# The beginning of an attention stage: order of norm, sigma and key preparation, and how far ahead they run

## The chip, the cores and the metric

The kernel runs on one core of a Trainium2 chip. A core has five engines that run their own instruction streams: TensorE (PE, matmuls; PEld is its weight load), VectorE (DVE), ScalarE (ACT), GpSimd (POOL) and SyncE (SP, which here only issues DMAs). ScalarE issues DMAs too. The metric is the device time of one execution in microseconds; the figure for a kernel is the median of its runs. One execution was recorded by the hardware profiler.

## The reference

A block of four residual stages on x of shape (2, 2048, 256) in float32: causal attention with 16 heads of 16, a mixture-of-experts feed-forward, a small gated stage, and the feed-forward once more, each on a layer norm of x. The change lies in the first stage only:

```python
def sn_dense(x, W, u, sigma_param):
    v = W @ u
    v = v / norm(v)
    u2 = W.T @ v
    u2 = u2 / norm(u2)
    sigma = einsum('c,cd,d->', v, W, u2)
    return x @ (sigma_param[0] / sigma * W)

h = layernorm(x)
q, k, v = split(sn_dense(h, W_qkv, u_qkv, sigma_qkv), 3)
att = einsum('bhqd,bhkd->bhqk', q, k) * hd ** -0.5
att = softmax(where(causal == 0, big_neg, att))
x = x + sn_dense(einsum('bhqk,bhkd->bhqd', att, v), W_proj, u_proj, sigma_proj)
```

sigma is a scalar per weight matrix; the kernel works out one factor sigma_param / sigma for qkv and one for proj, and applies it where results leave PSUM.

## The kernel before

x is held in eight chunks of 512 tokens (`X[0..7]`, four a batch). Attention works in **units** (batch, chunk, head group of 4 heads), 32 of them, in the list `units`. Names: `b`, `c`, `g`; `LAST` is chunk 0 of batch 1, which comes last in its batch and is prepared during the last chunk of batch 0.

For each chunk: `stat_steps` (lines 103 to 108) takes mean and variance on VectorE and 1/sqrt by a `pow` on GpSimd; `norm_steps` (L116) writes the normed tokens `xn` with four instructions, on GpSimd in attention; `flip_steps` (L126, L129) transposes them on PE into `xnT` by two PSUM banks, copied by ScalarE.

For each unit: `prepare` makes one PSUM bank of queries and keys (`psk`, L267), ScalarE writes the queries `qT` (L277, scaled by `fq`) and the keys to `sk` (L279), and SyncE copies the keys by four small DMAs into their place in a `kT` tile (L286), which GpSimd has filled with a constant row pattern the first time that it is used (L282). For group 0 of a chunk `prepare` begins with norm and transposes. `make_v` (L293, L298) makes the values of a chunk.

`Maxima` finds each query's largest score: matmuls `psm` (L333), reduced by VectorE (L342 on the diagonal, L347 elsewhere). `shift` (L351 to L358) puts the negated maximum into a row of `qT` by a transpose on VectorE and four DMAs. `softmaxes` then repeats the scores as `st` (L378), ScalarE takes exp (L382, `pt`), GpSimd clears what lies above the diagonal (L385, the mask selects), `values` multiplies with the values (`o`, L397), ScalarE copies out (L406) and GpSimd accumulates (L408). `finish` (L415 to L421) divides, `project` (L436 to L451) multiplies with W_proj and adds to x.

The main loop of attention emits all this in an order written out in the source: in each turn (`tick`) one step of the softmax of unit `na` and one step of the maxima of a later unit `nm`, with one step of the preparation of unit `nm` + 1 and of the statistics two units ahead of the chunk's need put between, and one DMA of the list `later` (loads of chunks 2 to 7, then zeros written to DRAM for a later stage). `ready` lets a softmax begin LAG turns after its maxima. `manual_schedule` makes the emitted order the order on each engine; ahead of it, a scheduler of the framework chose the order.

`spectral` works out a factor: two reductions of W times u on VectorE (L205), matmuls with one column (`psr`, L211), sums by a matmul with ones (`pss`, L224), and a chain of one-column operations on VectorE with one `pow` on GpSimd (L228 to L233). For qkv it stands behind the norm and the transposes of the first chunk and ahead of its first `psk`; for proj it is emitted at one place, at the end of the maxima of unit 1.

PSUM: four single banks (`ps_m`) serve `flip`, `psk`, `psm`, `psv`, `o` and the rest in turn, two double ones (`ps_st`) serve `st`.

The loads at the start: chunks 0 and 1 of x on SyncE's queue, W_qkv, u_qkv and sigma_qkv on ScalarE's.

Of the kernel before, what the change touches and what calls it, by code (L numbers as in the profile page):

```python
# [8 lines left out]
F32 = mybir.dt.float32  # L9
# [7 lines left out]
P = 128  # L17
D = 256
# [5 lines left out]
CH = 512  # L24
NB = CH // P
NCH = N // CH
# [15 lines left out]
WORDS = -(-EB // FW)  # L42
QTS = 6
KTS = NG * (NCH + 1)
LOW = -3e38
LAG = 3

# [2 lines left out]
def hybrid_block(  # L50
# [34 lines left out]
    def load_x(c):  # L85
        return X[c], x[c * CH:(c + 1) * CH, :].rearrange("(n p) d -> p n d", p=P)

    for c in range(2):
        nc.sync.dma_start(*load_x(c))

    ident = const.tile([P, P], F32, tag="ident", name="ident")
    make_identity(nc, ident)
# [19 lines left out]
    def norm_steps(xc, xn, nm, stats=None, eng=None):  # L112

        mv, rs = stats or (yield from stat_steps(xc, nm))
        for i in range(NB):
            (eng or nc.vector).tensor_scalar(  # L116
                xn[:, i, :], xc[:, i, :], mv[:, i, 0:1], rs[:, i:i + 1], ALU.subtract, ALU.mult
            )
        yield 1
# [16 lines left out]

    with tc.tile_pool(name="aw", bufs=1) as aw, ExitStack() as aw_ctx:

        maskq = aw.tile([P, CH], F32, tag="maskq", name="maskq")
        nc.gpsimd.memset(maskq, 0.0)  # L140
        nc.gpsimd.affine_select(
# [26 lines left out]
        KT = []  # L168
        for i in range(KTS):
            t = aw.tile([P, CH], F32, tag=f"kT{i}", name=f"kT{i}")  # L170
            KT.append(t)

        V = []
# [19 lines left out]
            return w, u, sp  # L193

        loaded = load_w(wqkv, uqkv, sqkv, 3 * D, "qkv")
        w_qkv = loaded[0]
        ones = aw.tile([P, P], F32, tag="ones", name="ones")
        nc.gpsimd.memset(ones, 1.0)

        def spectral(w, u, sp, cols, nm, bank):  # L200

            n = cols // P
            v = aw.tile([P, 2], F32, tag=f"v_{nm}", name=f"v_{nm}")
            for c in range(2):
                nc.vector.tensor_tensor_reduce(  # L205
                    wide(f"t_{nm}_{c}")[:, 0:cols], w[:, c, :], u, 1.0, 0.0, ALU.mult, ALU.add, v[:, c:c + 1]
                )
            ps = bank(f"psr_{nm}")
            for m in range(n):
                for c in range(2):  # L210
                    nc.tensor.matmul(  # L211
                        ps[:, m:m + 1], w[:, c, m * P:(m + 1) * P], v[:, c:c + 1],
                        start=c == 0, stop=c == 1,
                    )
            r = aw.tile([P, n], F32, tag=f"r_{nm}", name=f"r_{nm}")
            nc.vector.tensor_copy(r, ps[:, 0:n])

            s = aw.tile([P, 2], F32, tag=f"s_{nm}", name=f"s_{nm}")
            nc.vector.tensor_mul(v, v, v)
            nc.vector.tensor_mul(r, r, r)  # L220
            nc.vector.reduce_sum(s[:, 0:1], v, axis=AX.X)
            nc.vector.reduce_sum(s[:, 1:2], r, axis=AX.X)
            ps = bank(f"pss_{nm}")
            nc.tensor.matmul(ps[:, 0:2], ones, s, start=True, stop=True)  # L224

            f = aw.tile([P, 1], F32, tag=f"f_{nm}", name=f"f_{nm}")
            ru = aw.tile([P, 1], F32, tag=f"ru_{nm}", name=f"ru_{nm}")
            nc.vector.reciprocal(f, ps[:, 0:1])  # L228
            nc.vector.tensor_mul(f, f, ps[:, 1:2])
            nc.gpsimd.tensor_tensor(ru, f, nhalf[:, 0:1], ALU.pow)  # L230
            nc.vector.tensor_mul(f, f, ru)
            nc.vector.reciprocal(f, f)
            nc.vector.tensor_mul(f, f, sp)  # L233
            return f

        with ExitStack() as ac:
            xnp = ac.enter_context(tc.tile_pool(name="xnp", bufs=1))
# [7 lines left out]
            ps_m = ac.enter_context(tc.tile_pool(name="ps_m", bufs=4, space=PSUM))  # L245

            xnT, kT, qT, otok = {}, {}, {}, {}
            factors, nk, stats = {}, [0], {}

            order = [[0, 1, 2, 3], [1, 2, 3, 0]]  # L250
            LAST = (1, 0)
# [1 line left out]
            def bank(nm):  # L253
                return ps_m.tile([P, CH], F32, tag="mm", name=nm)

            def prepare(b, c, g):

                if g == 0:
                    xn = xnp.tile([P, NB, D], F32, tag="xn", name=f"xna_{b}_{c}")
                    yield from norm_steps(  # L260
                        X[b * NCH + c], xn, f"a{b}_{c}", stats.pop((b, c)), nc.gpsimd
                    )
                    t = xnT[b, c] = xtp.tile([P, 2, CH], F32, tag="xnT", name=f"xnTa_{b}_{c}")
                    yield from flip_steps(xn, t, bank, f"a{b}_{c}")
                ps = bank(f"psk_{b}_{g}_{c}")
                for d in range(2):
                    nc.tensor.matmul(  # L267
                        ps, w_qkv[:, d, g * P:(g + 1) * P], xnT[b, c][:, d, :],
                        start=d == 0, stop=d == 1,
                    )  # L270

                held = (b, c) == LAST
                qT[b, g, c] = qtp.tile(
                    [P, CH], F32, tag=f"qT{g}" if held else "qT", name=f"qT_{b}_{g}_{c}",
                    bufs=1 if held else QTS,
                )
                nc.scalar.activation(qT[b, g, c], ps, AF.Identity, scale=factors["q"])  # L277
                sk = skp.tile([P, CH], F32, tag="sk", name=f"sk_{b}_{g}_{c}")
                nc.scalar.activation(sk, ps, AF.Identity, scale=factors["k"])  # L279
                t = kT[b, g, c] = KT[nk[0] % KTS]  # L280
                if nk[0] < KTS:
                    nc.gpsimd.tensor_copy(t, kbias.to_broadcast([P, CH]))  # L282
                nk[0] += 1
                for j in range(4):
                    o = 32 * j + HD
                    nc.sync.dma_start(t[o - HD:o, :], sk[o:o + HD, :])  # L286
                yield
# [164 lines left out]

            units = [(b, c, g) for b in range(B) for c in order[b] for g in range(NG)]

            def preparations(n):

                todo = [units[n + 1]] if n + 1 < len(units) else []
                todo = [u for u in todo if u[:2] != LAST]
                if units[n][:2] == (0, NCH - 1):
                    todo.append((*LAST, units[n][2]))  # L460
                return (
                    (s for u in todo for s in prepare(*u)),
                    sum(4 if u[2] == 0 else 1 for u in todo),
                )


            ahead = {}
            for n in range(len(units)):
                for u in ([units[n + 1]] if n + 1 < len(units) else []) + [
                    (*LAST, units[n][2])  # L470
                ] * (units[n][:2] == (0, NCH - 1)):
                    if u[2] == 0 and (u[:2] != LAST or n < NG * NCH):
                        ahead[n - 2] = u[:2]

            def statistics(b, c):
                stats[b, c] = yield from stat_steps(X[b * NCH + c], f"a{b}_{c}", True)

            def make_vs(b, c):

# [21 lines left out]

            ready, mx, sm, behind = {}, None, None, None
            nm, na = 0, 0

            ac.enter_context(tc.manual_schedule())
            for _ in statistics(*units[0][:2]):
                pass
            first = prepare(*units[0])
            for _ in range(3):
                next(first)  # L510
            f = factors["k"] = spectral(*loaded, 3 * D, "qkv", bank)
            factors["q"] = aw.tile([P, 1], F32, tag="fq", name="fq")
            nc.vector.tensor_mul(factors["q"], f, qsel)
            for _ in first:
                pass
            for t in V:
                nc.gpsimd.memset(t, 1.0)
            loaded = load_w(wproj, uproj, sproj, D, "proj")
            w_proj = loaded[0]
            coming, steps, stat = iter(()), 0, iter(())  # L520
            while na < len(units) or due or behind:
                cols, n_m = CH, CH
                run_a = na < len(units) and ready.get(na, tick[0] + 1) <= tick[0]
                run_m = nm < len(units) and nm - na < QTS - 1
                if run_a:
                    u = units[na]
                    if sm is None:
# [39 lines left out]
                                after(5 + k, project, u[0], u[1], i, box)  # L567
                if run_m:
                    small_set = n_m <= 256 or not run_a
                    if steps and (small_set or steps == 4 or mx.left <= steps + 1):  # L570
                        next(coming, None)
                        steps -= 1
                    elif small_set:
                        next(stat, None)
                    if nm == 1 and not mx.left:
                        factors["p"] = spectral(*loaded, D, "proj", bank)
                    if later:
                        nc.sync.dma_start(*later.pop(0))
                    if not mx.left:
                        shift(*w, mx.part, nmax[nm % 2])  # L580
                        ready[nm] = tick[0] + LAG
                        mx, nm = None, nm + 1
# [702 lines left out]
```

## Time and profile before

| | |
|---|---|
| median of 3 runs | 2157.02 us (2152.82 to 2159.84) |
| profiled execution | 2150.73 us, its span 2148.8 us |
| busy: PE, weight loads | 2026.7 us (94%), 1091.1 us (51%) |
| busy: DVE, ACT, POOL | 1384.1 us (64%), 1074.9 us (50%), 872.9 us (41%) |
| chain that ended last, by engine | PE 80%, DVE 7%, POOL 4%, issue 4%, ACT 3%, DMA 1% |
| mean granted clock of TensorE | 0.979 |
| attention, its last `exp` | about 1172 us |
| first statistics, first transpose, first `psm` | 7.78, 13.45, 32.93 us |

The profile gives for each engine the time in which it was busy, in stretches that can be chosen; for groups of instructions their number, busy time and the mean of one; and for each wait what ended it ("<-"). The chain that ended last is followed back from the last instruction to what released it, step by step. The granted clock is the share of its full rate that PE was given. A busy PE isn't PE at its peak, since matmuls are pipelined.

### The profile page before, as it was taken

The page shows a single profiled execution, that of the slowest core. Times are in us where ns is not written, and L with a number is a line of the kernel's source. Part 1 is how long each engine was busy: PE and PEld are TensorE (multiplying, and loading weights), DVE is VectorE, ACT ScalarE, POOL GpSimd, SP SyncE. Part 2 cuts the span into 40 slices and gives each one's busy share as a digit, 9 for nine tenths or more (in the row PEclk, how much of TensorE's full clock was granted, in tenths as well). Part 3 has the DMA queues.
Part 4 walks back from the last instruction along what each step waited for, and adds up shares of the span by engine and source line. Part 5 has one row for each costly group of instructions (what it writes and reads, how often), then busy time and mean ns, then how long its engine had stood idle before and what let it go on. Part 6 is the DMA issues. An engine that isn't in the chain of part 4 may idle for free.

```text
span 2148.8 us, 36170 instructions
## 1 busy us (share of the span) xinstructions
PE 2026.7 (94%) x11840; PEld 1091.1 (51%) x11840; DVE 1384.1 (64%) x3424; ACT 1074.9 (50%) x1566; POOL 872.9 (41%) x1157
## 2 busy tenths in 40 slices
PE   6899999999999999999999999999999999999993
PEld 3444444444444444444444566665656566655662
DVE  2567777777676777777871455545777368763643
ACT  0437577757776757767876122233353234341330
POOL 3325344524444434434445263603432753336305
PEclk9899999999999999999999999999999999999997
DMA  2111110000000000000000511323210332103524
GB/s 93 48 49 36 45 51 16 7 6 6 3 7 6 6 4 4 6 4 4 2 2 1 217 61 64 136 76 118 84 40 25 114 112 85 35 30 131 173 73 122
DMA packets 87587, 113.04 MB, mean 53 GB/s; under 512 B 16368, under 2 KB 75120, under 8 KB 87280
## 3 DMA queue, kind: packets, MB, share of 16 engines
q1 hardware_dynamic: 74000, 75.60, 11.1%
q0 software_dynamic: 12288, 33.57, 4.7%
q8 instruction: 101, 1.65, 0.3%
q10 hardware_dynamic: 1120, 1.57, 0.2%
q14 instruction: 78, 0.64, 0.1%
HBM read 54.59 MB, written 51.64 MB: 49 GB/s over the span
## 4 chain that ended last, share of the span: by engine, by line
PE 80%; DVE 7%; POOL 4%; issue 4%; ACT 3%; DMA 1%; DVEq 0%; SPq 0%; POOLq 0%; ACTq 0%
PE st L378 15%; PE o L397 13%; PE psm L333 13%; PE eu L1060 10%; PE s L986 7%; PE ed L1084 5%; PE sy L1003 4%; PE psk L267 3%; PE tr L1045 2%; PE psz L936 1%; PE psj L446 1%; POOL xs L868 1%; PE psv L293 1%; DVE junk L342 1%; PE psl L736 1%
## 5 line engine op out<-in xcount | busy, mean ns | idle before, releaser
L382 ACT ACTIVATE pt<-st 128x1024 f32<-128x1024 f32 (+3 forms) x640 | 555.8, 895 | 189.8 <-PE psm L333 129.9
L333 PE MATMUL psm<-kT,qT 32*128 32x512 f32 (+3 forms) x2560 | 627.1, 570 | 15.0 <-DMA kT<-sk 8.9
L378 PE MATMUL st<-qT,kT 32*128 32x512 f32 (+3 forms) x2560 | 610.7, 557 | 1.3 <-ACT pt L382 1.3
L347 DVE TENSOR_REDUCE part<-psm 128x1 f32<-128x512 f32 x768 | 477.4, 682 | 121.5 <-PE psm L333 117.3
L408 POOL TENSOR_TENSOR oa<-oa,op 128x512 f32<-128x512 f32 (+3 forms) x288 | 312.8, 1086 | 454.4 <-ACT op L406 454.4
L378 PEld LDWEIGHTS st<-qT,kT 32*128 32x128 f32 x2560 | 266.1, 186 | 225.9 <-ACT pt L382 137.8
L342 DVE CUSTOM_DVE_ANT_0 junk<-psm,maskq 128x384 bf16<-128x384 f32 (+3 forms) x512 | 250.8, 490 | 112.0 <-PE psm L333 47.7
L333 PEld LDWEIGHTS psm<-kT,qT 32*128 32x128 f32 x2560 | 276.1, 186 | 86.2 <-issue 27.1
L397 PE MATMUL o<-pt,v 128*32 128x512 f32 (+3 forms) x2560 | 304.2, 545 | 12.1 <-DVE part L347 5.6
L1060 PE MATMUL eu<-we,turned 128*128 x560 | 263.7, 593 | 0.0
L1067 ACT ACTIVATE es<-ea 128x256 f32<-128x256 f32 x156 | 65.0, 417 | 357.9 <-DVE ea L1065 357.8
L986 PE MATMUL s<-xT_f,ws 128*128 128x512 f32 x512 | 231.4, 595 | 0.0
L895 POOL DMA_INDIRECT yg<-ys,slot x128 | 128.1, 1001 | 234.3 <-DVE x L908 74.0
L385 POOL TENSOR_SCALAR_AFFINE_SELECT pt<-pt 128x256 f32<-128x256 f32 x256 | 102.3, 407 | 211.6 <-ACT pt L382 207.7
L406 ACT COPY op<-o 128x512 f32<-128x512 f32 (+3 forms) x288 | 148.3, 515 | 64.1 <-PE o L397 48.8
L1065 DVE TENSOR_TENSOR ea<-eu,be 128x512 f32<-128x512 f32 x156 | 107.4, 688 | 111.0 <-PE eu L1060 110.4
L1084 PE MATMUL ed<-we,turned 128*128 x624 | 162.6, 383 | 14.5 <-ACT turned L1050 14.5
L397 PEld LDWEIGHTS o<-pt,v 128*32 128x32 f32 x2560 | 52.5, 108 | 218.0 <-DVE part L347 123.4
L1084 PEld LDWEIGHTS ed<-we,turned 128*128 128x128 f32 x624 | 116.2, 190 | 87.9 <-issue 48.3
L868 POOL DMA_INDIRECT xs<-xn_f,slot x128 | 124.7, 974 | 85.1 <-DVE slot L822 57.9
L986 PEld LDWEIGHTS s<-xT_f,ws 128*128 128x128 f32 x512 | 94.8, 191 | 102.0 <-issue 95.4
L1060 PEld LDWEIGHTS eu<-we,turned 128*128 128x128 f32 x560 | 97.6, 191 | 75.0 <-issue 73.1
(266 smaller groups left out, 2111.0 us busy)
## 6 DMA issues: line engine op xcount, KB each, us to landing
xs<-xs SPq DMA_DIRECT2D x156, 128.0 KB
ys<-ey SPq DMA_DIRECT2D x156, 128.0 KB
xs<-zeros SPq DMA_DIRECT2D x78, 128.0 KB
we<-in_we_dram SPq DMA_DIRECT2D x8, 768.0 KB
x<-in_x_dram SPq DMA_DIRECT2D x8, 512.0 KB
kT<-sk SPq DMA_DIRECT2D x128, 32.0 KB
out_dram<-x SPq DMA_DIRECT2D x8, 512.0 KB
be<-in_be_dram SPq DMA_DIRECT2D x1, 3072.0 KB
```

The costliest lines, as they stand in the source:

```text
L333: nc.tensor.matmul(ps[:, :n], self.q[r, i * P:(i + 1) * P], kT[b, g, kc][r, :n], start=True, stop=True,)
L342: nc.vector.tensor_tensor_reduce(junk[:, :n], ps[:, :n], maskq[:, CH - n:], 1.0, LOW, ALU.add, ALU.max, m,)
L347: nc.vector.reduce_max(m, ps[:, :n], axis=AX.X)
L378: nc.tensor.matmul(st[:, i, off:], k[r, ks], q[r, off:], start=True, stop=True)
L382: nc.scalar.activation(pt[:, :, off:], st[:, :, off:], AF.Exp)
L397: nc.tensor.matmul(o[32 * j:32 * j + 32, off:], V[kb // NB][:, kb % NB, 4 * g + j, :], pts[j // 2][:, j % 2, off:], start=True, stop=True,)
L406: nc.scalar.copy(t[:, off:], o[:, off:])
L408: nc.gpsimd.tensor_tensor(a[:, off:], a[:, off:], t[:, off:], ALU.add)
L868: ins = nc.gpsimd.indirect_dma_start(out=XS[b], out_offset=bass.IndirectOffsetOnAxis(ap=slots[f, b][:, k, n:n + 1], axis=0), in_=xhat[f, b ...
L986: nc.tensor.matmul(ps, w[:, d, cs], xT[:, d, :], start=d == 0, stop=d == 1)
L1060: nc.tensor.matmul(ps, t[:, 1, d * P:(d + 1) * P], we_s[:, bass.ds(v + d * CH, CH)], start=d == 0, stop=d == 1,)
L1084: nc.tensor.matmul(ps[:, 0:D], t[:, 0, d * P:(d + 1) * P], we_s[:, bass.ds(v + 2 * CH + d * D, D)], start=d == 0, stop=d == 1,)
```

## The change

- x's chunk 0 is loaded in two halves of two blocks each; chunk 1 goes to ScalarE's queue, behind W_qkv, u_qkv and sigma_qkv.
- The written-out order begins at the start of attention and not ahead of the main loop.
- The first eight `kT` tiles are filled at the start.
- `spectral` becomes a generator of three steps (reductions; `psr` and sums; `pss` and the rest). For qkv the first step comes ahead of the first norm and the second ahead of the transposes; for proj one step is taken in each of three turns of unit 2.
- The norm moves from `prepare` into `statistics`, so a chunk is normed where its statistics are done; the first chunk's by VectorE, the others by GpSimd.
- While fewer than EARLY (8) units have begun, `prepare` runs for unit `nm` + 2 and not `nm` + 1 (units 0 and 1 both ahead of the loop), and maxima may be four units ahead of the softmax, not five.

```diff
+KTE = 8
+EARLY = 8
...
-    for c in range(2):
-        nc.sync.dma_start(*load_x(c))
+    for h in range(2):
+        t, src = load_x(0)
+        nc.sync.dma_start(t[:, 2 * h:2 * h + 2, :], src[:, 2 * h:2 * h + 2, :])
...
+        aw_ctx.enter_context(tc.manual_schedule())
...
             t = aw.tile([P, CH], F32, tag=f"kT{i}", name=f"kT{i}")
+            if i < KTE:
+                nc.gpsimd.tensor_copy(t, kbias.to_broadcast([P, CH]))
...
         loaded = load_w(wqkv, uqkv, sqkv, 3 * D, "qkv")
+        nc.scalar.dma_start(*load_x(1))
...
-        def spectral(w, u, sp, cols, nm, bank):
+        def spectral(w, u, sp, cols, nm, bank, got):
...
+            yield 1
             ps = bank(f"psr_{nm}")
...
             nc.vector.reduce_sum(s[:, 1:2], r, axis=AX.X)
+            yield 1
             ps = bank(f"pss_{nm}")
...
-            return f
+            got(f)
+            yield 1
...
                 if g == 0:
-                    xn = xnp.tile([P, NB, D], F32, tag="xn", name=f"xna_{b}_{c}")
-                    yield from norm_steps(
-                        X[b * NCH + c], xn, f"a{b}_{c}", stats.pop((b, c)), nc.gpsimd
-                    )
+                    xn = normed.pop((b, c))
...
-                if nk[0] < KTS:
+                if KTE <= nk[0] < KTS:
                     nc.gpsimd.tensor_copy(t, kbias.to_broadcast([P, CH]))
...
+            def coming_to(n):
+
+                if n == EARLY:
+                    return []
+                k = n + 1 + (n < EARLY)
+                return units[k:k + 1]
+
             def preparations(n):
 
-                todo = [units[n + 1]] if n + 1 < len(units) else []
-                todo = [u for u in todo if u[:2] != LAST]
+                todo = [u for u in coming_to(n) if u[:2] != LAST]
...
-                    sum(4 if u[2] == 0 else 1 for u in todo),
+                    sum(3 if u[2] == 0 else 1 for u in todo),
...
-                        ahead[n - 2] = u[:2]
+                        ahead[n - 2 + (u[:2] == LAST)] = u[:2]
 
             def statistics(b, c):
-                stats[b, c] = yield from stat_steps(X[b * NCH + c], f"a{b}_{c}", True)
+                s = yield from stat_steps(X[b * NCH + c], f"a{b}_{c}", True)
+                xn = normed[b, c] = xnp.tile([P, NB, D], F32, tag="xn", name=f"xna_{b}_{c}")
+                if not (b or c):
+
+                    next(sigma)
+                yield from norm_steps(
+                    X[b * NCH + c], xn, f"a{b}_{c}", s, nc.gpsimd if b or c else nc.vector
+                )
...
-            ac.enter_context(tc.manual_schedule())
+            def scaled(f):
+                factors["k"] = f
+                factors["q"] = aw.tile([P, 1], F32, tag="fq", name="fq")
+                nc.vector.tensor_mul(factors["q"], f, qsel)
+
+            sigma = spectral(*loaded, 3 * D, "qkv", bank, scaled)
             for _ in statistics(*units[0][:2]):
                 pass
+            next(sigma)
             first = prepare(*units[0])
-            for _ in range(3):
-                next(first)
-            f = factors["k"] = spectral(*loaded, 3 * D, "qkv", bank)
-            factors["q"] = aw.tile([P, 1], F32, tag="fq", name="fq")
-            nc.vector.tensor_mul(factors["q"], f, qsel)
+            next(first)
+            for _ in sigma:
+                pass
             for _ in first:
                 pass
+            for _ in prepare(*units[1]):
+                pass
...
+            sigma = spectral(*loaded, D, "proj", bank, lambda f: factors.update(p=f))
...
-                run_m = nm < len(units) and nm - na < QTS - 1
+                run_m = nm < len(units) and nm - na < QTS - 1 - (nm < EARLY)
...
-                    if steps and (small_set or steps == 4 or mx.left <= steps + 1):
+                    if steps and (small_set or steps == 3 or mx.left <= steps + 1):
                         next(coming, None)
                         steps -= 1
                     elif small_set:
                         next(stat, None)
-                    if nm == 1 and not mx.left:
-                        factors["p"] = spectral(*loaded, D, "proj", bank)
+                    if nm == 2:
+                        next(sigma, None)
```

In the new order PE runs `psr`, the first four transposes, `pss`, the other four, `psk` of unit 0, `psk` of unit 1, then the first `psm`.

More of the change, by code (lines that the diff above doesn't have):

```diff
@@ L247, in hybrid_block @@
             xnT, kT, qT, otok = {}, {}, {}, {}
-            factors, nk, stats = {}, [0], {}
+            factors, nk, normed = {}, [0], {}
             order = [[0, 1, 2, 3], [1, 2, 3, 0]]
@@ L468, in hybrid_block @@
             for n in range(len(units)):
-                for u in ([units[n + 1]] if n + 1 < len(units) else []) + [
-                    (*LAST, units[n][2])
-                ] * (units[n][:2] == (0, NCH - 1)):
+                for u in coming_to(n) + [(*LAST, units[n][2])] * (units[n][:2] == (0, NCH - 1)):
                     if u[2] == 0 and (u[:2] != LAST or n < NG * NCH):
-                        ahead[n - 2] = u[:2]
+                        ahead[n - 2 + (u[:2] == LAST)] = u[:2]
             def statistics(b, c):
-                stats[b, c] = yield from stat_steps(X[b * NCH + c], f"a{b}_{c}", True)
+                s = yield from stat_steps(X[b * NCH + c], f"a{b}_{c}", True)
[5 more added lines that the diff above has]
+                )
             def make_vs(b, c):
```

## The prediction

> **What bounds the kernel now.** I read the page first (TensorE, PE, is busy 94% of the span and carries 80% of the chain that ended last), then the busy time by stretches, to find where PE is not full.
>
> ```profile
> 0.00:130.00 130.00, 98.17 (x524) 50.92 (x528) 58.40 (x228) 38.59 (x63) 45.73 (x77) 0.88 0.22 70
> 130.00:870.00 740.00, 723.32 (x5428) 333.52 (x5420) 550.92 (x1330) 501.44 (x678) 306.00 (x382) 0.99 0.06 16
> ```
>
> Columns: length, busy time of PE, weight loads, VectorE, ScalarE, GpSimd, then granted clock. From 130 us on attention leaves PE idle for 16.7 us in 740; before that it is idle for 31.8 us in 130. So the change works where time is to be had, and what it saves there is kept, because all later work stands behind it on a full PE. Next the timeline and the chain of waits of that stretch:
>
> ```profile
> 12.16 4.85 POOL L116 TENSOR_SCALAR xna<-x,lnmv_a,lnrs_a 128x256 f32<-128x256 f32 x4
> 18.19 5.12 PE L211 MATMUL psr_qkv<-v_qkv,w_qkv 128*128 128x1 f32 x24
> 24.40 3.76 PE L267 MATMUL psk<-xnTa,w_qkv 128*128 128x512 f32 x4
> 32.93 2.84 PE L333 MATMUL psm<-kT,qT 32*128 32x512 f32 x8 [4.76 <-DMA kT<-sk]
> ...
> 68.01 1.81 PE psr_proj L211 x8
> ...
> 70.44 0.60 PE pss_proj L224 x2
> ...
> 92.45 0.33 PE L126 MATMUL flip_a<-ident,xna 128*128 128x128 f32 x1 [0.88 <-POOL xna L116]
> ...
> 109.28 1.62 PE L333 MATMUL psm<-kT,qT 32*128 32x256 f32 x5 [4.09 <-DMA kT<-sk]
> ```
>
> Four losses are seen: the head runs in series up to 32.93; sigma of proj holds PE between 68.0 and 70.95; the second chunk's transposes wait for GpSimd's norm, four times; the second chunk's first keys wait 4.09 us for their copy. Between them the clock drops:
>
> ```profile
> 44.00:53.50 9.50, 9.32 (x26) 6.06 (x24) 3.74 (x19) 0.00 (x0) 0.00 (x0) 0.50 0.68 227
> 64.50:74.00 9.50, 7.56 (x41) 4.44 (x44) 5.66 (x33) 2.59 (x4) 2.89 (x6) 0.50 0.32 105
> 95.00:98.00 3.00, 3.00 (x17) 1.22 (x16) 0.62 (x1) 1.18 (x2) 1.21 (x3) 0.50 0.00 0
> 109.00:115.00 6.00, 5.72 (x22) 2.79 (x23) 1.73 (x8) 1.07 (x2) 1.36 (x3) 0.50 0.10 29
> ```
>
> Before 43.7 us the record says 1.0, but four psk matmuls take 3.76 us there and 1.98 at 55.75: PE is at half rate from its start to 53.5.
>
> **The change, part by part.** Unit means one (batch, chunk, head group); the maxima of unit n are psm, its softmax st, exp and o.
>
> *x in halves, x1 to ScalarE's queue.* All statistics start at 7.78 and end with lnve at 10.2 (four blocks of 0.57 us, then 0.17). In halves, two blocks run before the second half lands. [...] I take **1.1**: lnve ends at 9.07. ScalarE issues one more copy of about 0.5 us ahead of a table load that nobody needs before 17.
>
> *Sigma of qkv beside the norm, norm on VectorE, kT fills early.* The two reductions (0.96 us each) run on VectorE while GpSimd does pow (1.75): 9.07 + 1.85 = 10.9. PE starts psr there and not behind the transposes: 10.95 + 5.1 = 16.1. The norm costs four times the row of the same operation in the later stages,
>
> ```profile
> L696 DVE TENSOR_SCALAR xn_f<-x,lnmv_f,lnrs_f 128x256 f32<-128x256 f32 x64 | 22.6, 408 | 9.8 <-POOL lnrs_f L692 9.8
> ```
>
> 1.6 us in place of 4.85, done at 12.6 under psr. Then flip 0.9 (17.0), pss 0.6, flip 0.8 (18.4), psk 3.7 at half rate: 22.1 against 28.2. The factor is ready 2.2 us after pss (19.8), so it is hidden. The eight kT fills (0.6 us each, 4.7 us) stand on GpSimd between 2.6 and 7.4, before pow can start; without that cover they would cost 4.7. From psk to the first psm it is 4.75 us as now (ScalarE, then SyncE's issue, then 1.94 of copy): first psm at **26.8, a gain of 6.1**. psk of unit 1 (3.7) falls into that wait.
>
> *Units 0 and 1.* Now 32.93 to 70.95. psk of units 2 and 3 stand where those of 1 and 2 stood. VectorE needs for a unit 4 x (0.84 + 0.71 + 0.58 + 0.44) = 10.3 us; unit 0 gets also 2.4 us of statistics (from unit 1) and 1.6 of v. [...] The trace: in 36 to 43, with PE busy 6.87 of 7 us on psk and psm, durations stay at half rate; it opens at 53.5 after 3.7 us of psv without a gap. [...] I take 18.6: unit 1 starts at 45.4, not 53.72. Unit 1 drops its 2.4 us of statistics (14.3 to 11.9) and the 2.95 us of sigma of proj: unit 2 starts at 57.3, not 70.95. **Gain so far 13.7** (11 to 16).
>
> *Units 2 to 4.* Without waits and at full rate unit 3 costs 16.15 - 3.0 (four waits for the norm) - 1.5 (half of 95 to 98) - 1.2 (transposes) = 10.4. Unit 2 now costs 14.5 with one psk; it becomes 10.4 + 1.2 transposes + 1.2 psr and pss of proj + 1.9 psk = 14.7: **-0.2**. The norm of chunk 1 (pow 1.0, then 4.85 on GpSimd) stands ahead of the first mask selects, but there GpSimd idles 27.7 us now. Sigma's three steps put 1.2 us of reductions and 13 small operations of about 0.1 on VectorE. Unit 3 becomes 10.4 + 1.9 psk + 0.5 of statistics that show: **+3.3**. From 101.65 on the psk of the new chunk (1.9) and the wait for its keys (4.1) fall away: **+6.0**. The half rate of 109 to 115 with psk in it: 3.0 + 1.1 less the 1.9 of the psk that comes in its place: **+2.2**. Sum 13.7 + 11.3 = 25.
>
> *What is late next.* VectorE is within a microsecond of PE in units 0 to 3 (10.3 against 10.4), and four PSUM banks couple them, so not all of it is kept: I take 85%, **21**.
>
> *Later chunks.* The order of psm, st and o is the same before and after; only transposes, psk and norms move earlier. The norm (4.84 on GpSimd) stood one accumulate ahead of mask selects at 197 and 343, and an o waited for it (0.84 each); at 556 it cost 2.9 us of waits, and 1.5 of half clock after it. Now mostly two accumulates or none stand between, some four to seven microseconds. Gain **2** (from -3, if each of the six norms delays a select by 0.5, to +6). Running at most four units ahead instead of five in the first eight moves no instruction of this order.
>
> Total **23**. The profiled execution takes 2150.7 us (span 2148.8), so 2127.7; the median of the runs, 2157.0, lies 6.3 above it, so 2134.
>
> **The rivals.**
> 1. *VectorE becomes the bound in units 0 to 3.* For it: its 10.3 us a unit, plus statistics, v and sigma, equals PE's. Against it: now it is busy 58 of 130 us. Then the head (6.1), sigma's stall and the key wait (4.1) partly remain saved: gain 8 to 14, time 2146.
> 2. *The change does little.* The clock stays shut longer since units run bound by VectorE with PE half idle, and the head is set by the landing of x and the weights: 6.1 falls to about 4 and half-rate loss eats the rest. Gain under 6.5: about 2153. Against it: the waits at 68, 91 and 105 go in any case.
> 3. *Slower: GpSimd's norm blocks mask selects.* Each norm is 4.84 us in front of selects and accumulates, and exp results are held until the select is done. Seven norms at full length would cost 34 us against 23 gained: 2168. It decides once a norm costs PE more than 3.3 us on average. Against it: the new order has a select directly behind the norm only for chunks 1 and 2.
>
> **How the numbers follow.** Forecast 0.66 (gain 16 to 30), rival 1 0.22, rival 2 0.07, rival 3 0.05. About 0.3% (6.5 us) is what a measurement tells from no change. Faster 0.88, same 0.07, slower 0.05. The range takes in rival 1 in most of its width and the open ends of clock (±2.3), x (±1) and later chunks (-5, +4): 2124 to 2148.
>
> **What would show it.** In the changed profile: psr ahead of the transposes, first psm near 26.8; unit 2's first st near 57; no wait of transposes for the norm of chunk 1 and no key wait of 4 us; PE idle under 10 us between its first instruction and 110 (now 18); the same PE share after that. Wrong would be: first psm after 30, granted clock of 0.5 over more of the first 110 us than now, or o waiting for selects behind each norm.

## The result and the profile after

| | before | after |
|---|---|---|
| median of 6 runs each | 2154.03 us (2149.11 to 2159.84) | 2118.88 us (2117.58 to 2120.48) |
| profiled execution, its span | 2150.73, 2148.8 us | 2117.58, 2115.8 us |
| mean granted clock | 0.979 | 0.983 |

The ratio is 0.9835 (95% interval 0.982 to 0.985): faster by 35 us by the medians, by 33 us between the two profiled executions. The forecast was 2134 us, a gain of 23, with a range down to 2124. The direction was right; the gain is half as large again as forecast.

The busy time by stretches of the changed kernel (length, then busy time of PE, weight loads, VectorE, ScalarE, GpSimd, granted clock, DMA share, GB/s):

```profile
0.00:130.00 130.00, 111.05 (x649) 59.43 (x650) 81.15 (x281) 46.75 (x76) 51.76 (x86) 0.93 0.26 80
130.00:835.00 705.00, 692.50 (x5281) 320.64 (x5283) 528.44 (x1273) 492.71 (x663) 295.55 (x366) 1.00 0.05 15
0.00:110.00 110.00, 91.20 (x550) 49.26 (x551) 64.36 (x241) 40.23 (x67) 43.80 (x76) 0.92 0.27 84
```

In the first 130 us PE is idle for 19.0 us, where it was 31.8; behind that it is idle for 12.5 us in 705, where it was 16.7 in 740. So the change also worked past the stretch that it was aimed at. The timeline of the head (start, duration, engine, line, operation, tiles, count, idle time before it and what ended it):

```profile
4.78 0.43 DVE L106 BATCH_NORM_STATS2 lnst_a<-x 128x6 f32<-128x256 f32 x1 [2.42 <-DMA x<-in_x_dram]
8.17 0.43 DVE L106 BATCH_NORM_STATS2 lnst_a<-x 128x6 f32<-128x256 f32 x1 [2.22 <-DMA x<-in_x_dram]
9.38 0.17 DVE L110 TENSOR_SCALAR lnve_a<-lnmv_a 128x4 f32<-128x4 f32 x1
11.41 4.86 PE L220 MATMUL psr_qkv<-v_qkv,w_qkv 128*128 128x1 f32 x22 [0.29 <-DVE v_qkv L213]
11.42 1.38 DVE L119 TENSOR_SCALAR xna<-x,lnmv_a,lnrs_a 128x256 f32<-128x256 f32 x4
16.13 1.09 PE L129 MATMUL flip_a<-ident,xna 128*128 128x128 f32 x4
18.31 4.85 PE L275 MATMUL psk<-xnTa,w_qkv 128*128 128x512 f32 x8
27.57 2.62 PE L341 MATMUL psm<-kT,qT 32*128 32x512 f32 x8 [4.41 <-DMA kT<-sk]
```

`psr` stands ahead of the transposes, the norm is over long before them, and all eight `psk` (the matmuls of units 0 and 1) run in one go: at half rate they would take 7.5 us, at full rate some 4 (four of them took 3.76 us at 24.40 and 1.98 at 55.75 in the kernel before), so the clock opened on the way. The first three last about 1.0 us each, the others 0.59. Then PE waits 4.41 us for the keys' copy. The matmul timeline of units 2 to 4:

```profile
65.59 0.95 PE L220 MATMUL psr_proj<-v_proj,w_proj 128*128 128x1 f32 x8
...
71.10 0.28 PE L234 MATMUL pss_proj<-s_proj,ones 128*128 128x2 f32 x2
...
88.19 0.76 PE L341 MATMUL psm<-kT,qT 32*128 32x256 f32 x2
```

Sigma of proj no longer stops PE, and the second chunk's first `psm` (109.28 before) has no wait for its keys. The clock, in the stretches where it was low:

```profile
27.70:34.50 6.80, 6.67 (x15) 2.56 (x18) 2.80 (x8) 0.36 (x1) 0.00 (x0) 0.50 0.04 10
34.50:37.90 3.40, 3.06 (x14) 1.20 (x11) 2.29 (x9) 0.91 (x2) 0.00 (x0) 1.00 0.09 19
37.90:48.10 10.20, 9.82 (x27) 6.52 (x26) 6.13 (x28) 0.00 (x0) 5.61 (x5) 0.50 0.68 215
```

Half rate begins where the wait for the keys ends, and comes a second time at 37.9 us. Unit 0 therefore still runs mostly at half rate (17.0 of its 20.8 us), and then the clock stays open until 730 us; before, there were further falls at 64, 95, 109, 559 and 764 us.

Where the time comes from, by the start of a unit's first `psm` in both traces:

| start of | before | after | gain so far | forecast |
|---|---|---|---|---|
| unit 0 | 32.93 | 27.57 | 5.4 | 6.1 |
| unit 1 | 53.72 | 48.33 | 5.4 | 8.3 |
| unit 2 | 70.97 | 59.75 | 11.2 | 13.7 |
| unit 4 (chunk 1 of batch 0) | 109.28 | 88.19 | 21.1 | 22.8 |
| unit 5 | 138.70 | 115.66 | 23.0 | 25, kept 21 |
| unit 9 | 258.50 | 231.84 | 26.7 | |
| unit 15 | 539.45 | 512.18 | 27.3 | |
| unit 16 (chunk 1 of batch 1) | 598.32 | 565.43 | 32.9 | |
| last `o` of attention | 1173.26 | 1139.70 | 33.6 | 23 |

After attention nothing more is gained. The question for the runs was what brings the 10.5 us behind unit 5, for which I had forecast 2, and what each part of the beginning is worth.

### The profile page after: what moved, and what is told of

Read it like the earlier page. It is cut to its first block, busy times and chain, and to the rows that moved or that the text cites. A ratio compares the mean times of both kernels' runs of the same rounds, so it can differ in the third digit from the quotient of the medians.

```text
span 2115.8 us, 36162 instructions
## 1 busy us (share of the span) xinstructions
PE 2010.0 (95%) x11840; PEld 1087.9 (51%) x11840; DVE 1386.0 (66%) x3428; ACT 1075.5 (51%) x1566; POOL 870.5 (41%) x1153
## 4 chain that ended last, share of the span: by engine, by line
PE 82%; DVE 7%; ACT 3%; issue 3%; POOL 3%; DMA 2%; DVEq 0%; SPq 0%; POOLq 0%; ACTq 0%
PE st L386 15%; PE o L405 13%; PE psm L341 13%; PE eu L1085 10%; PE s L1011 7%; PE ed L1109 5%; PE sy L1028 4%; PE psk L275 3%; PE tr L1070 3%; PE psz L961 1%; PE psj L454 1%; POOL xs L893 1%; PE psv L301 1%; DVE junk L350 1%; PE psl L761 1%
## 5 line engine op out<-in xcount | busy, mean ns | idle before, releaser
L405 PE MATMUL o<-pt,v 128*32 128x512 f32 (+3 forms) x2560 | 301.2, 541 | 11.2 <-DVE part L355 6.7
```

The source lines that it names most:

```text
L405: nc.tensor.matmul(o[32 * j:32 * j + 32, off:], V[kb // NB][:, kb % NB, 4 * g + j, :], pts[j // 2][:, j % 2, off:], start=True, stop=True,)
```

## The experiments

"Trace loss" is the last `o` of attention in the run's trace less that of the changed kernel (1139.70 us). The kernel before had a median of 2151.33 us beside runs 1, 2, 4 and 5, and 2152.29 beside runs 6 to 8, against 2154.03 beside the changed kernel. The changed kernel itself did not run beside these eight, so a difference of its median from theirs is uncertain by 2 to 3 us; the losses and gains at single places are read from the traces.

**1. The late norm.** The changed kernel, but from chunk (0,2) on the norm goes back into `prepare`, right ahead of the transposes, on GpSimd:

```diff
-                    xn = normed.pop((b, c))
+                    if (b, c) in normed:
+                        xn = normed.pop((b, c))
+                    else:
+                        xn = xnp.tile([P, NB, D], F32, tag="xn", name=f"xna_{b}_{c}")
+                        yield from norm_steps(
+                            X[b * NCH + c], xn, f"a{b}_{c}", stats.pop((b, c)), nc.gpsimd
+                        )
...
+                if b or c > 1:
+                    stats[b, c] = s
+                    return
...
```

> The changed kernel with one part undone: from the third chunk on the norm is again a step of prepare, just ahead of the transposes. Theory A (the part of the gain that the prediction missed comes from the norm standing earlier in the later chunks): it loses 5 to 9 us of the 33, most of it in chunk (1,1), and time lies at 2124 to 2128; transposes wait for the norm again. Rival B (the later chunks gain because the early part shifts everything, or by chance of the clock): loss of 0 to 2 us, 2119 to 2121.

Measured: 2129.61 us (2123.38 to 2131.89), ratio 0.9891 (0.987 to 0.9911); trace loss 7.55. At unit 6 this run was 1.9 us ahead (its unit 0 met a better clock, see run 7), so its trace loses 9.4 us from there on. Of these, 7.5 us lie where the late norm stands: 0.9 in unit 6, 1.3 in unit 11 and 5.3 in unit 15, the turn to unit 16. The other 1.9 can't be put down to it: two falls of the clock, in units 9 and 13, cost 1.7 each and unit 21 gives 1.6 back, but runs 5 (unit 9), 6 and 7 (unit 13) have the same falls with an early norm. The profiled execution is the longest of the four, and another 7 us of its time lie behind attention. So this is theory A in its place and size, with a time above its range. At the turn to unit 16 the timeline reads:

```profile
532.68 4.83 POOL L119 TENSOR_SCALAR xna<-x,lnmv_a,lnrs_a 128x256 f32<-128x256 f32 x4
...
533.95 0.33 PE L129 MATMUL flip_a<-ident,xna 128*128 128x128 f32 x1 [0.40 <-POOL xna L119]
535.16 0.33 PE L129 MATMUL flip_a<-ident,xna 128*128 128x128 f32 x1 [0.88 <-POOL xna L119]
536.37 0.33 PE L129 MATMUL flip_a<-ident,xna 128*128 128x128 f32 x1 [0.88 <-POOL xna L119]
537.57 0.33 PE L129 MATMUL flip_a<-ident,xna 128*128 128x128 f32 x1 [0.87 <-POOL xna L119]
537.93 0.58 ACT L132 COPY xnTa<-flip_a 128x512 f32<-128x512 f32 x1 [3.89 <-PE flip_a L129]
539.99 1.29 DVE L361 TENSOR_REDUCE part<-psm 128x1 f32<-128x512 f32 x2 [6.08 <-PE psm L347]
```

PE ran its instructions in the emitted order. Each transpose waits for its quarter of the norm, 3.0 us in sum, and the `psm` queued behind them wait too, so VectorE stands idle for 6.08 us. The clock then falls from 537.8 to 541.2, which takes another 1.7 (half of its 3.4). The kernel before had the same waits at this turn, and a longer fall (559.2 to 566.0); two of its four transposes:

```profile
557.28 0.33 PE L126 MATMUL flip_a<-ident,xna 128*128 128x128 f32 x1 [0.41 <-POOL xna L116]
558.49 0.33 PE L126 MATMUL flip_a<-ident,xna 128*128 128x128 f32 x1 [0.88 <-POOL xna L116]
```

In the changed kernel the turn has no such wait; the busy time of six microseconds of it, and its transposes:

```profile
526.00:532.00 6.00, 5.82 (x64) 3.42 (x60) 3.40 (x19) 3.51 (x8) 3.30 (x6) 1.00 0.02 4
```

```profile
527.00 0.66 PE L129 MATMUL flip_a<-ident,xna 128*128 128x128 f32 x4
...
529.95 0.66 PE L129 MATMUL flip_a<-ident,xna 128*128 128x128 f32 x4
```

**2. The norm alone.** The kernel before, with the norm moved into `statistics` (GpSimd) and nothing else changed:

```diff
-                stats[b, c] = yield from stat_steps(X[b * NCH + c], f"a{b}_{c}", True)
+                s = yield from stat_steps(X[b * NCH + c], f"a{b}_{c}", True)
+                xn = normed[b, c] = xnp.tile([P, NB, D], F32, tag="xn", name=f"xna_{b}_{c}")
+                yield from norm_steps(X[b * NCH + c], xn, f"a{b}_{c}", s, nc.gpsimd)
...
```

> The kernel before with one part of the change alone: the norm of each chunk moves into statistics, on GpSimd as before (the first chunk's too). Theory A: chunk (0,1) gains its 3.0 us of waits and some 1.5 of half clock, the later chunks 6 to 9: gain 10 to 13 us over the kernel before, 2141 to 2144 where that has 2154. Rival B (only together with preparing two ahead): gain under 4 us.

Measured: 2133.43 us (2131.42 to 2140.36), ratio 0.9928 (0.9905 to 0.995), against the kernel before. The gain is 18 us by the medians and 19.3 in attention's trace (last `o` at 1153.99). Of this, 5.3 us is the phase of the clock in unit 0, which has the same PE instructions in both (run 7); the other 14 lies just above the theory. Half of it, 6.9 us, is there at unit 5, and 7.0 comes behind it. The turn from unit 15 to 16 takes 53.27 us here, 58.87 in the kernel before, 58.56 in run 1 and 53.25 in the changed kernel: this step alone accounts for it, with or without the rest. It also takes most of the wait for the second chunk's keys (4.09 us before), though units are still prepared only one ahead:

```profile
99.66 1.04 PE L330 MATMUL psm<-kT,qT 32*128 32x256 f32 x3 [0.86 <-DMA kT<-sk]
```

**3. The late norm on VectorE.** Run 1 with `nc.vector` in place of `nc.gpsimd`. It ran on another chip, together with the two runs under 9. There the kernel before took 2242.03 us and the changed kernel 2206.70; the extra time lies behind attention, at a mean granted clock of 0.94 in place of 0.98 from 1160 us on. So this run is compared with the changed kernel on that chip.

> Chunks from (0,2) on are normed right before their transposes, as before the change, but by VectorE (4 x 0.4 us) instead of GpSimd (4.85 us). Theory A (what cost the kernel before in the later chunks is GpSimd's length of the norm in front of the transposes): most of the 7.5 us that the late norm on GpSimd loses by the end of attention comes back; loss against the changed kernel 0 to 3 us there, time about 2119 to 2122. Theory B (the place costs, whichever engine norms, because the transposes then follow the norm at once): loss 5 to 8 us, time 2124 to 2129.

Measured: 2218.59 us (2216.87 to 2221.07), 11.9 us more than the changed kernel there; the last `o` comes 12.55 us later than in its trace. Theory A falls; theory B holds. The wait has only changed its place. Busy time and timeline of the turn from unit 15 to 16:

```profile
531.00:537.00 6.00, 3.76 (x42) 1.96 (x40) 5.25 (x20) 2.03 (x5) 2.64 (x5) 1.00 0.01 3
```

```profile
532.99 2.31 DVE L119 TENSOR_SCALAR xna<-x,lnmv_a,lnrs_a 128x256 f32<-128x256 f32 x4
...
535.23 0.24 DVE L432 RECIPROCAL rc<-pso 128x16 f32<-128x16 f32 x1
535.51 0.42 DVE L435 TENSOR_TENSOR otok<-pso,rc 128x256 f32<-128x256 f32 x1
...
536.08 0.45 PE L347 MATMUL psm<-kT,qT 32*128 32x128 f32 x2 [2.24 <-DVE otok L435]
```

The norm now stands ahead of the division that frees a PSUM bank, and the next `psm` waits 2.24 us for that bank; PE is busy 3.76 us of 6. The turns of chunks cost 1.5 to 2.4 us each, 7.7 in sum over four of them, which is theory B's range; most of the rest comes with falls of the clock at 357 and 740 us, which the changed kernel's trace of that chip does not have there. How much of that is the norm's is not shown: the changed kernel's first trace has a fall at 731 us.

**4. One unit ahead.** The changed kernel with `EARLY = 0`: preparation one unit ahead, maxima five. Unit 1 is still prepared ahead of the loop, and unit 0 prepares nothing.

> The changed kernel with EARLY at 0: every unit is prepared one ahead, the norm stays early. Theory A: the wait for the second chunk's keys comes back (4.1 us), with half clock after it (about 2), and the statistics of the second chunk stand in unit 1, where they show (2.4), not in unit 0, where they are covered: loss 6 to 9 us, 2125 to 2128. Rival B (VectorE bounds units 0 to 3 anyway): loss under 3 us, 2122 at most.

Measured: 2127.08 us (2125.22 to 2127.23), 8.2 more than the changed kernel; trace loss 6.8. The time is theory A's, but its largest term did not come: the wait for the second chunk's keys is 0.84 us, not 4.1.

```profile
89.98 0.67 PE L341 MATMUL psm<-kT,qT 32*128 32x256 f32 x2 [0.84 <-DMA kT<-sk]
```

Unit 0 is 4.6 us shorter, since another unit's `psk` and the second chunk's statistics no longer stand in it; units 1 to 3 take 6.6 more, with these in them and the clock at half from 54.9 to 61.7. Unit 8, which prepares for unit 9 again, takes 2.2 more. The rest comes and goes with falls of the clock.

**5. Sigma of proj in one block**, at the end of unit 1's maxima, with the reductions:

```diff
-                    if nm == 2:
-                        next(sigma, None)
+                    if nm == 1 and not mx.left:
+                        for _ in sigma:
+                            pass
```

> The changed kernel with sigma of proj in one block at the end of unit 1's maxima. Theory A: PE stands 3 us on psr, pss and their waits, and the clock may fall: loss 3 to 6 us, 2122 to 2125. Rival B (unit 1 became shorter only since the statistics left it): loss under 1 us.

Measured: 2122.02 us (2119.29 to 2123.19), 3.1 more; trace loss 4.39. Theory A. Unit 1 takes 14.15 us in place of 11.42, close to the 2.95 of stall that the prediction read in the trace of before. Unit 2 takes another 2.6 more, and the clock is at half from 58.8 to 69.0 in it. That the trace loss is no more than 4.39 is due to a unit 0 that is 3.9 us shorter (run 7).

**6. The loads as before**: both chunks whole on SyncE's queue.

```diff
-    for h in range(2):
-        t, src = load_x(0)
-        nc.sync.dma_start(t[:, 2 * h:2 * h + 2, :], src[:, 2 * h:2 * h + 2, :])
+    for c in range(2):
+        nc.sync.dma_start(*load_x(c))
...
-        nc.scalar.dma_start(*load_x(1))
```

> The changed kernel with the loads as before: x0 in one piece, x1 behind it on SyncE's queue. Read at the first psm (27.57 in the changed kernel), since the clock's phase blurs the rest. Prediction's term: 1.1 us later. Rival (the whole x0 lands as early as the second half does, and the reductions are the bound): under 0.5 us later.

Measured: 2119.74 us (2117.86 to 2123.91), not told apart from the changed kernel. The statistics end 0.73 us later (10.11 in place of 9.38) and `psk` begins 0.73 later, but the eight `psk` then last 4.11 us in place of 4.85, and the first `psm` comes at 27.48 against 27.57. The rival's number came, but not by its reason: the delay does reach `psk`, and the clock takes it back, since it opens in the second `psk` here and in the third in the changed kernel. With another phase of the clock some 0.7 us of the expected 1.1 could show.

**7. The head.** Two runs: the first norm on GpSimd (`nc.gpsimd` for every chunk); and the same with the matmuls of sigma behind the transposes, as in the kernel before:

```diff
-                if not (b or c):
-                    next(sigma)
...
-            next(sigma)
             first = prepare(*units[0])
             next(first)
+            next(first)
```

> The changed kernel with the first norm on GpSimd again, all else left. Theory A: psr of qkv (11.4 to 16.3) covers it, since GpSimd would end at 11.4 + 4.85 = 16.3: first psm at most 0.5 us later. Rival B (VectorE's shorter norm is what shortens the head): 3 us later.

> The changed kernel with the first norm on GpSimd and psr of qkv behind the transposes, as before; halves of x, early kT fills and two ahead stay. Theory A: norm and psr are in series again, first psm 4 to 5 us later, at 31.5 to 32.5, time 2122 to 2125. Rival B (order of psr without effect): under 1.5 us later.

Measured: 2117.58 us (2117.0 to 2118.74) with the norm on GpSimd, and 2123.27 us (2121.38 to 2126.14) with the old order too. The timeline of the first, GpSimd's norm among it:

```profile
11.39 4.86 PE L220 MATMUL psr_qkv<-v_qkv,w_qkv 128*128 128x1 f32 x22 [0.29 <-DVE v_qkv L213]
11.47 4.85 POOL L119 TENSOR_SCALAR xna<-x,lnmv_a,lnrs_a 128x256 f32<-128x256 f32 x4
...
16.11 1.09 PE L129 MATMUL flip_a<-ident,xna 128*128 128x128 f32 x4
```

The transposes begin at 16.11 here and at 16.13 in the changed kernel, since `psr` holds PE until then: behind `psr`, the move of the first norm to VectorE is worth nothing (theory A). With the norm on GpSimd the order is worth the head's gain: with the old one the first `psm` comes at 33.32, later than in the kernel before (32.93), and a little later than theory A had it.

```profile
12.56 0.48 PE L129 MATMUL flip_a<-ident,xna 128*128 128x128 f32 x1 [12.56 <-POOL xna L119]
...
17.30 5.12 PE L220 MATMUL psr_qkv<-v_qkv,w_qkv 128*128 128x1 f32 x24
...
33.32 1.19 PE L341 MATMUL psm<-kT,qT 32*128 32x512 f32 x5 [4.15 <-DMA kT<-sk]
```

The old order with the norm on VectorE, where the short norm might count, did not run. Of the 5.75 us, 3.2 are left at unit 1, because the clock takes part of them back.

That clock is visible across the traces. From the first `psm` to unit 1, with the same PE instructions, it takes 20.8 us in the kernel before and 15.5 in run 2; 20.8 in the changed kernel, 20.3 in run 6, 18.3 in run 1 and 16.8 in run 5. Half rate comes in pieces of 3.4 us (run 1, from 537.8), 6.8 and 10.2 (the changed kernel, from 27.7 and 37.9) or 13.7 (run 8, from 34.7), and how they fall on unit 0 differs.

**8. The wait for the first keys filled.** The values of the first chunk (16 `psv`), which needed PE in unit 0, are made in the wait for the keys:

```diff
+            make_v(0, 0, 0)
+            make_v(0, 0, 2)
...
-                        if w[2] == 0 and w[0] == 0:
+                        if w[2] == 0 and w[0] == 0 and nm:
```

> The changed kernel with one addition: the first chunk's two banks of values are made right behind the keys of unit 1, in PE's wait for the first key copies (27.57 is the first psm, PE is idle from 23.2), and no longer inside unit 0. Theory A (unit 0 and the start of unit 1 are set by PE's clock and by psv standing between psm): PE has no gap before the first psm, the clock stays open, and unit 0 takes 15 to 17 us in place of 20.8; time 2113 to 2116. Rival B (unit 0 is set by VectorE's own work): gain under 2 us.

Measured: 2117.32 us (2116.95 to 2122.07), ratio 0.9839 (0.9817 to 0.9861): not told apart, as rival B had it, though unit 0 is shorter than even theory A had it. The trace shows what becomes of it:

```profile
23.11 3.62 PE L301 MATMUL psv<-w_qkv,xnTa 128*128 128x256 f32 x16
27.50 1.74 PE L341 MATMUL psm<-kT,qT 32*128 32x512 f32 x8 [0.77 <-DMA kT<-sk]
...
39.60 3.40 PE L341 MATMUL psm<-kT,qT 32*128 32x512 f32 x8 [0.70 <-DVE part L350]
```

The wait is 0.77 us, the clock stays open (1.00 from 23 to 34.7 us), and unit 1 starts at 39.60, 8.7 us earlier. Then it is at half rate from 34.7 to 48.4, though PE is recorded busy 3.68 of the 3.70 us before; 3.7 us are left from unit 3 on and 3.96 at the last `o`, after a fall at 349 us that the changed kernel's trace lacks and without the one that it has at 731. In this execution a fall from 1680 to 1687 us, which the changed kernel's profile does not have, takes most of the rest: both profiled executions end at the same time (2117.61 and 2117.58).

**9. Filled wait, first norm on GpSimd** (runs 7 and 8 together), **and the changed kernel once more**, on one chip:

> The changed kernel with the first chunk's values in the wait ahead of the first psm, and the first norm on GpSimd. Theory A (filling that wait with PE work that is needed anyway is worth 3 to 4 us by the end of attention, as the trace of the version with the values alone shows, and the engine of the first norm is indifferent): last o of attention 3 to 4.5 us earlier than in the changed kernel, time 1 to 4 us less. Theory B (half-clock intervals decide, the place of the values only shifts them): last o within 2 us of the changed kernel's, times not told apart.

> The changed kernel itself, for two things. Time beside the other two on one chip: 2117 to 2121 us expected. And its unit 0: theory A (the phase of the clock intervals against the start decides how long unit 0 takes): from the first psm to the first of unit 1 another length than 20.8 us, between 15.5 and 20.8. Theory B (the order of instructions decides): 20.8 within 0.3 us.

Measured: 2201.14 us (2199.91 to 2203.89), ratio 0.9826 (0.9811 to 0.9842), and 2206.70 us (2205.07 to 2208.48), ratio 0.9845 (0.9831 to 0.9859); in the trace the last `o` comes 3.68 us earlier. The first has theory A: its runs all lie below those of the changed kernel, 5.5 us by the medians, more than the 1 to 4 expected, though the intervals of the ratios overlap. It is the fastest of the four versions on that chip. The repeat took 20.5 us from first `psm` to unit 1: theory B by its number, though the same PE instructions took 16.8 and 18.3 elsewhere. Its time was not within the expected range because this chip takes longer behind attention (run 3).

## Why the prediction came out as it did

- **What bounds the kernel.** Right for the first 130 us. But I took the 16.7 us of idle PE behind it as given, and the change took 4.2 of these too.
- **x in halves.** 1.1 us forecast, which no run shows: statistics end 0.7 us earlier than with the loads of before, and in run 6 the phase of the clock hid that at the first `psm`. Two whole blocks would have been gained with the second half there when the whole load was (7.78); it could be used at 8.17.
- **Sigma beside the norm.** 6.1 forecast, 5.4 measured; with the norm on GpSimd, all of it comes from the order of PE's queue. The price of VectorE's norm (1.6 forecast, 1.38 measured) did not matter: run 7 shows that `psr` covers the 4.85 us of GpSimd as well. The early `kT` fills stayed in every run, so what they are worth is not shown.
- **Unit 0.** I took 18.6 us, an estimate, and counted 2.2 us of gain; it took 20.8, as before. The clock did open in the `psk` of units 0 and 1 (the first three about 1.0 us each, the others 0.59). My reading of the trace of before was wrong: in the kernel before, PE was not at half rate all the way to 53.5. The record's 1.0 between 40.3 and 43.7 is true, and the same `psm` shows it, three of them on the two sides of 40.3:

```profile
39.47 1.01 PE L333 MATMUL psm<-kT,qT 32*128 32x384 f32 x3
40.27 0.53 PE L333 MATMUL psm<-kT,qT 32*128 32x384 f32 x3
```

I also left out that a wait for the keys is left behind `psk`. I had filled 3.7 us of it with `psk` of unit 1 at half rate; at the opened clock these were over sooner, PE stood 4.41 us, and at the end of that wait the clock fell (0.50 from 27.7 to 34.5). In run 8, with 0.77 us of the wait left, it did not fall there. No run shows the 18.6 as the price of the unit: the same PE instructions took 15.5 to 20.8 us from trace to trace.

- **Unit 1, sigma of proj, units 2 to 4.** From unit 1 to unit 2 forecast 5.4, measured 5.8; sigma's stall is confirmed by run 5. From unit 2 to unit 5 forecast 11.3, measured 11.8. The terms hold to about half a microsecond together, but not each for its reason: 3.2 of the 4.1 us of the key wait go with the early norm alone (runs 2 and 4), not with preparing two ahead.
- **What is late next.** "I take 85%" was a discount for VectorE that nothing in the trace bore out: 23.0 of 25 were there at unit 5, and the 2 that lack are unit 0's 2.2 and 0.7 of the head, less 0.9 that units 1 to 4 gained beyond their forecast. Rival 1 did not come, nor rival 2.
- **Later chunks, the step that failed.** "Gain 2 (from -3 [...] to +6)" measured 10.5 from unit 5 on, beyond its upper end. The waits for the norm that I had listed come to 6.1 us: 0.84 each at 197 and 343 us, 2.9 of waits and 1.5 of clock at the turn to unit 16. The runs show these and a little more: the early norm alone gains 7.0 us from unit 5 on (run 2), the late one loses 7.5 at its turns (run 1), and run 3 shows that the engine's length is not the reason. What took 6 down to 2 was a delay of mask selects that I set against it, and it did not come. Between 120 and 1130 us PE waited for selects twice in the kernel before, and never in the changed one. Before (us in total, times, longest us):

```profile
PE o L397 <- POOL pt L385: 1.6, 2, 0.8
```

The turn to unit 16 was also priced too low, 4.4 against 5.3 to 5.6 measured: I counted the transposes' own waits and 1.5 us for the clock. Behind the transposes the `psm` wait too, VectorE runs dry (6.08 us in run 1), and the clock in the kernel before was at half for 6.8 us. The turns to units 8 and 12 gained 1.6 and 2.5 us, but 1.0 of that had been lost in unit 6 and 2.2 went again in unit 12. Of the 3 us or so that the norm does not explain, 2.2 come in unit 8, where preparation pauses, which I had overlooked in `coming_to`: at unit 5 the changed kernel has made one `psk` (1.9 us) more than before, and there it comes back.

- **Rival 3** (norms on GpSimd hold up mask selects) is refuted by the time itself, and by run 1: with the norm back in its old place the time is longer, not shorter.
- **The signs named.** `psr` ahead of the transposes, no norm wait and no key wait of 4 us in chunk 1, and 8.3 us of idle PE up to 110 us (110 less 10.5 ahead of its first matmul and 91.2 busy; under 10 forecast) all came; unit 2's first scores came 2.5 us later than forecast, by unit 0 and the head. "The same PE share after that" was wrong, and it is where the missing gain lies.

So the sum of the beginning, without the discount, was right to 2 us. The time fell below the range because the later term was taken at 2 and not allowed more than 6, and because the discount took 4 us off a sum of which only 2 failed to come. Another 3 us are the base: the forecast starts from 2157.0 us, the median of three runs, and with six it is 2154.0.

## What to carry to other kernels

An instruction that waits at the head of PE's queue can cost more than its own wait (3.0 us of waits, 5.3 lost at one turn): price it with what queues behind it, the engine that this starves (VectorE for 6.08 us), and a fall of the clock afterwards (3.4 us in run 1, 6.8 in the kernel before). Move the producer earlier; making it faster in the same place can just hold up something else (a PSUM bank for 2.24 us in run 3). Set a feared loss against a gain only where a trace shows a wait for it. In a stretch where the clock falls, look first for a wait of PE just ahead of the fall (4.41 us ahead of 27.57 here; with 0.77 us of it left in run 8 the clock stayed open there). A gain of a few microseconds is then judged by several traces at the same milestones, not by one.

## What the runs showed of the hardware

- **The falls of the clock.** In the traces of the kernel before and of the changed one they last 3.41, 6.83 or 10.24 us (save the fall that runs past the end of each), multiples of 3.413; in run 8 one lasts 13.7. Their phase against the kernel differs: the same PE instructions of unit 0 took 15.5 to 20.8 us.
- **VectorE beside GpSimd.** In run 3 a norm instruction of VectorE took 0.39 to 0.41 us alone, and up to 1.36 us beside an accumulate of GpSimd (two inputs; 1.27 us, 128x512, in four of the six late chunks, 0.84 and 1.00 us in the others). At the turn to unit 16 the four instructions of a norm took 2.31 us beside the accumulate of 1.00 us (128x384). No run tried the instruction in another form, so the cause is not shown.
- **Two halves of one load.** The halves of chunk 0, issued one behind the other on SyncE's queue, could be used 3.4 us apart (4.78 and 8.17), and the second no earlier than the whole load (7.78 in the kernel before, 7.85 in run 6).
- **An open point.** Why the clock fell at 34.7 us in run 8, with PE recorded busy 3.68 us of the 3.70 before, is not settled, nor why it fell again at 37.9 us in the changed kernel, with PE busy 3.06 us of the 3.40 before. The ends of matmuls are modelled, so short gaps between them may be missing from that count.
